# SS2D scan: the products with C made for two tiles at once, and two buffers shared

## The chip, the cores and the metric

The kernel runs on one core of one Trainium2 chip. The metric is the time of one whole execution in microseconds (us), the median of several runs. Before the change it is 18144.38 us (three runs, 18138.38 to 18144.7).

The core has five engines that run at the same time, each with its own queue of instructions that it works off in order: TensorE (PE in the profile; its weight loads are PEld), VectorE (DVE), ScalarE (ACT), GpSimd (POOL) and SyncE (SP), whose queue here issues the transfers between HBM and the on-chip memory.

## The reference

The network has four layers on eight images of 56 x 56 positions and 128 channels. Layers 0, 2 and 3 are deformable convolutions with a feed-forward part; the change does not touch them. Layer 1 is a vision state-space block. Its core is a selective scan with Di = 256 channels, N = 16 states per channel and K = 4 directions (rows forward, columns forward, and both reversed):

```
def step(h, t):
    dt_t, u_t, B_t, C_t = t
    h = h * jnp.exp(dt_t[..., None] * A) + (dt_t * u_t)[..., None] * B_t[:, :, None, :]
    y = jnp.einsum('bkdn,bkn->bkd', h, C_t)
    return (h, y)
...
_, ys = jax.lax.scan(step, h0, ts)
ys = ys + Ds.reshape(K, Di)[None, :, :, None] * xs
...
y = _ln(y, out_norm_w, out_norm_b)
y = y * jax.nn.silu(z)
y = jnp.einsum('bhwd,cd->bhwc', y, out_proj_w)
x = x + y
xm = _ln(x, norm2_w, norm2_b)
h = jax.nn.gelu(jnp.einsum('bhwc,fc->bhwf', xm, fc1_w) + fc1_b)
x = x + jnp.einsum('bhwf,cf->bhwc', h, fc2_w) + fc2_b
```

Here dt is a softplus of a projection, and B and C are rows per state that all channels share. So for each image, direction, channel and state, a first-order recurrence runs over 3,136 positions; each h is multiplied by C and summed over the 16 states.

## The kernel before

*Tiles and steps.* A step is one image, one direction and one chunk of SC = 784 positions: 8 images x 4 directions x 4 chunks = 128 steps, the directions in the order 1, 3, 0, 2. The 256 x 16 pairs of channel and state do not fit 128 partitions; a step is cut into 32 tiles t, each of 32 channels by 4 states. The tile's channel group is cg (8 of them) and its state group is sg (4 of them), and t = 4 cg + sg. "A group" in what follows is the four tiles of one cg. That makes 4,096 tiles in all.

*One tile's work*, in `scans` (L1323):
- `decay` (L1366): ScalarE computes dA = exp(dt * A) into one of two PSUM buffers.
- `spread` (L1358): once per group TensorE copies dt*x into PSUM (tile dtu, one buffer).
- `inputs` (L1371): u = dtu * B. For sg 0, 1 and 2 VectorE does it (two buffers u); for sg 3 GpSimd does it from on-chip memory, into the single buffer up.
- L1471: VectorE runs the recurrence (a tensor-tensor scan) into h, which has three buffers of one tile.
- L1474: ScalarE copies the last column into st, the carry to the next chunk (not in the last chunk of a direction).
- L1476: GpSimd multiplies h by the rows of C into hc, which has six buffers.
- `add_sums` (L1395): TensorE sums hc over the states into the PSUM bank acc, two tiles at a time, three tiles later. `open_sums` and `close_sums` begin and empty acc every eight tiles.

*What sets the order.* The program is unrolled in Python, in the order in which `scans` writes it; a scheduler then orders the instructions of each engine by this priority and by when it expects their inputs and buffers to be ready. `tc.issue_after` keeps the sums behind the last `spread` on TensorE. Waits come from data and from buffers: a new use of a buffer waits until everything that read the old one is done. So the scan of tile t waits for the product of tile t - 3 (three buffers h), and the product of tile t waits for the sums of tile t - 6 (six buffers hc).

*Background work.* While step `at` is scanned, a generator `prepare` (L1265) makes the next step's dt, B and C, one piece at each tile with sg 1 or 2: projections on TensorE, then for each half of the channels the softplus as Relu(x) + Ln(1 + Exp(-|x|)) on ScalarE (L1288 to L1292, the logarithm in tile sp, the rest in tile dd, one buffer each), an add and a product on GpSimd (L1294 and L1296), and a transfer of dd to HBM (L1298). `fetch_dt` (L1309) and `fetch_row` (L1301) bring dt and the rows of B and C back, spread over partitions; B and C have five buffers of one tile each, and the rows for the next step are fetched at tiles 25, 28, 29, 30 (B) and 26, 29, 30, 31 (C). A queue of tasks advances by one piece at most tiles: `input_stage` (L1110) prepares the next image (norm, convolution, gate; it writes tile pre), and `output_stage` (L1182) finishes an image in 8 pieces of 392 positions: it centers y into tile yc (L1195), normalizes it (L1203), gates it on GpSimd (L1207), projects it, and runs the feed-forward part in tile pre.

Of the kernel before, what the change touches and what calls it, by code (L numbers as in the profile page):

```python
# [41 lines left out]
F32 = mybir.dt.float32  # L42
# [70 lines left out]
NCH = DI // 128  # L113
XD = RANK + 2 * NST

LC = 448
NLC = L // LC
RPC = LC // W
SC, SR = 784, 14
# [4 lines left out]
NF = FF // 128  # L124
# [865 lines left out]
class Vss:  # L990
# [191 lines left out]
    def output_stage(self, i, c):  # L1182
# [4 lines left out]
        nc.sync.dma_start(out=sg, in_=self.gates[i][:, NCH:, m * c : m * (c + 1)])  # L1187
        yield
        yield
        yc = self.bg.tile([128, NCH, m], F32, name="yc", tag="yc")  # L1190
        for h in range(NCH):
            ps = self.misc()
            for g in range(NCH):
# [24 lines left out]
        nc.scalar.copy(x, ps[:, :m])  # L1218
        yield
        xT = self.bg.tile([128, m], F32, name="xT", tag="xT")  # L1220
        pre = self.bg.tile([128, NF, m], F32, name="pre", tag="pre", padded_shape=[128, NF, LC])
        ps = self.misc()
        nc.tensor.matmul(ps[:, :m], lhsT=w["center"], rhs=x, start=True, stop=True)
        nc.scalar.copy(xT, ps[:, :m])
# [39 lines left out]
    def prepare(self, s, k, c):  # L1264

        nc, w = self.nc, self.w
        xs = self.part(self.xb, k, c)
        dbl = self.prep.tile([XD, SC], F32, name="dbl", tag="dbl")
        s["rows"] = self.dram.tile([NST, 2 * SC], F32, name="rows", tag="rows")
        s["dd"] = self.dram.tile([DI, 2 * SC], F32, name="dds", tag="dds")  # L1270
        for b in range(2):
            ps = self.misc()
            for ch in range(NCH):
                nc.tensor.matmul(ps[:XD, :SH].rearrange("p (a b) -> p a b", b=W), lhsT=w["xproj"][:, ch, k, :], rhs=xs[:, ch, SR // 2 * b : SR // 2 * (b + 1)], start=ch == 0, stop=ch == NCH - 1)
            yield
            nc.scalar.copy(dbl[:, SH * b : SH * (b + 1)], ps[:XD, :SH])
        nc.sync.dma_start(out=s["rows"].rearrange("n (x e) -> (n x) e", x=2), in_=dbl[RANK:])
        yield
        for h in range(NCH):
            dd = self.prep.tile([128, 2, SC], F32, name="dd", tag="dd")  # L1280
            sp = self.prep.tile([128, SC], F32, name="sp", tag="sp")

            bias = w["dt_b"][:, NCH * k + h : NCH * k + h + 1]
            for b in range(2):
                at = slice(SH * b, SH * (b + 1))
                ps = self.misc()
                nc.tensor.matmul(ps[:, :SH], lhsT=w["dt"][:, k, 128 * h : 128 * (h + 1)], rhs=dbl[:RANK, at], start=True, stop=True)
                nc.scalar.activation(sp[:, at], ps[:, :SH], AF.Abs, bias=bias)  # L1288
                nc.scalar.activation(dd[:, 0, at], ps[:, :SH], AF.Relu, bias=bias)
                yield  # L1290
            nc.scalar.activation(sp, sp, AF.Exp, scale=-1.0)
            nc.scalar.activation(sp, sp, AF.Ln, bias=1.0)  # L1292
            yield
            nc.gpsimd.tensor_add(dd[:, 0], dd[:, 0], sp)  # L1294
            yield
            nc.gpsimd.tensor_mul(dd[:, 1].rearrange("p (a b) -> p a b", b=W), dd[:, 0].rearrange("p (a b) -> p a b", b=W), xs[:, h])  # L1296
            yield
            nc.sync.dma_start(out=s["dd"][128 * h : 128 * (h + 1)], in_=dd.rearrange("p x e -> p (x e)"))  # L1298
            yield

    def fetch_row(self, s, x, sg):  # L1301

        name = "bc"[x]
        t = s[name, sg] = self.work.tile([128, SC], F32, name=name, tag=name, bufs=NSG + 1)
        r = s["rows"]
        src = bass.AP(tensor=r.tensor, offset=r.offset + TS * sg * 2 * SC + x * SC, ap=[[0, TC], [2 * SC, TS], [1, SC]])
        self.nc.sync.dma_start(out=t, in_=src)
# [15 lines left out]
    def scans(self):  # L1323
# [99 lines left out]
        decay(*units[0])  # L1423
        inputs(*units[0])
        st = ready = None
        group, late = [], deque()
        zeros = self.zeros()
        for now, (at, t) in enumerate(units):
            (i, k, c), s, (cg, sg) = steps[at], state[at], order[t]
            forward = k < 2  # L1430
            if t == 0:
                if at % NSC == 0:
                    st = self.prep.tile([128, NT], F32, name="st", tag="st", bufs=2)
                    nc.gpsimd.memset(st, 0.0)
                if at % (NDIR * NSC) == 0 and i + 1 < self.images:
                    tasks.append(self.input_stage(i + 1))
                ready = iter(())
                if at + 1 < len(steps):
                    if steps[at + 1][0] > i:
                        self.load_xb(i + 1)  # L1440
                    ready = self.prepare(state[at + 1], *steps[at + 1][1:])
            if t % (2 * NSG) == 0:
                late.append((now + 5, open_sums, (at, t)))
            while late and late[0][0] <= now:
                _, do, args = late.popleft()
                do(*args)
            if sg == 1:
                to = divmod(NCG * at + cg + 2, NCG)
                if to[0] < len(steps):
                    self.fetch_dt(state[to[0]], to[1])  # L1450
            if t in (3, 19):
                next(zeros, None)

            for x, when in enumerate(((25, 28, 29, 30), (26, 29, 30, 31))):
                if t in when and at + 1 < len(steps):
                    self.fetch_row(state[at + 1], x, when.index(t))
            if now + 1 < len(units):
                decay(*units[now + 1])
                if not on_pool(units[now + 1][1]):
                    inputs(*units[now + 1])  # L1460

                if sg == NSG - 3 and now + 3 < len(units):
                    spread(*units[now + 3])
            if now + 2 < len(units) and on_pool(units[now + 2][1]):
                inputs(*units[now + 2])
            if sg in (1, 2):
                next(ready, None)
            hh = self.work.tile([128, SC], F32, name="h", tag="h", bufs=3)
            step = 1 if forward else -1
            u, dA = s.pop(("u", t)), s.pop(("dA", t))  # L1470
            nc.vector.tensor_tensor_scan(hh[:, ::step], dA[:, :SC][:, ::step], u[:, ::step], st[:, t : t + 1], ALU.mult, ALU.add)  # L1471
            if c != (NSC - 1 if forward else 0):
                last = SC - 1 if forward else 0
                nc.scalar.copy(st[:, t : t + 1], hh[:, last : last + 1])  # L1474
            hc = self.work.tile([128, SC], F32, name="hc", tag="hc", bufs=6)
            nc.gpsimd.tensor_mul(hc, hh, s["c", sg])  # L1476
            group.append((order[t], hc))
            if t % 2:
                late.append((now + 3, add_sums, (at, group)))
                group = []  # L1480
                if t % (2 * NSG) == 2 * NSG - 1:
                    late.append((now + 5, close_sums, (at, t)))
            if sg or (i == self.images - 1 and k == 2):
                advance(1)
# [81 lines left out]
```

## Time and profile before

| | |
|---|---|
| median of the runs | 18144.38 us |
| the profiled execution | 18131.72 us |
| its span, first to last instruction | 18130.2 us |
| scan stage within it, about | 2,360 to 13,500 us |
| busy DVE / POOL / PE / ACT, whole span | 15374.0 / 11790.9 / 13876.0 / 10917.1 us |
| product hc (L1476) | 4,096 of 1.877 us, 7559.1 us |
| scan h (L1471) | 3,072 of 1.838 and 1,024 of 1.833 us |
| u on VectorE (L1379) and up on GpSimd (L1375) | 3,072 of 0.955, 1,024 of 1.860 us |
| dA on ScalarE (L1369) | 4,096 of 0.915 us |
| add and product of the preparation (L1294, L1296) | 256 each, of 1.862 and 2.056 us |
| gating of y (L1207) | 64 of 1.852 us |
| a step in the scan stage, 3,000 to 13,000 us | about 87 us (115 steps) |

How to read it: a line of a group gives the line of the kernel, the engine, the operation, output and inputs by tile name with their shapes, the count, then the busy time and mean duration in ns of one, and after the second bar the engine's idle time just before these instructions with what ended it ("<-POOL hc L1476 260.8": for 260.8 us the engine waited until GpSimd's product ended). Durations of neighbours overlap by some 0.05 to 0.1 us, so the distance from start to start is a little shorter than the mean duration. In a table of stretches the columns are the stretch, its length, busy time and count of PE, PEld, DVE, ACT and POOL, the granted TensorE clock, the DMA share and GB/s.

### The profile page before, as it was taken

To read this page: it belongs to the slowest core of one execution; us is meant where nothing else is said; L and a number is where in the kernel's file an instruction comes from. 1 tells how busy PE (TensorE), PEld (TensorE's weight loads), DVE (VectorE), ACT (ScalarE), POOL (GpSimd) and SP (SyncE) were. 2 spreads that over 40 slices of the span, in tenths; PEclk is the share of its full clock that TensorE was granted. 3 is DMA by queue.
4 is the path that set the end of the run, shared out by engine and by line. 5 is a ranking of instruction groups with operands and counts; after the bars stand their busy time and mean duration, and the time that the engine had idled before them with its cause. 6 is when DMAs were issued, how large, how long until landed. Compare 5 with 4: busy or idle time off the path is not lost. (4 is left out here: it accounts for less than half of the span.)

```text
span 18130.2 us, 255599 instructions
## 1 busy us (share of the span) xinstructions
PE 13876.0 (77%) x90059; PEld 6901.9 (38%) x90059; DVE 15374.0 (85%) x17784; ACT 10917.1 (60%) x19602; POOL 11790.9 (65%) x6462
## 2 busy tenths in 40 slices
PE   5777787688688688688788778778676888577777
PEld 4655422233232232232223223222134666455555
DVE  8888368998998998998998898899976887688886
ACT  4666555566566566566566566656554666456666
POOL 2221079998998998998998998999971111222221
PEclk7778888899899899899899899889886888677777
DMA  7777444444443443444443444444335777577777
GB/s 216 210 200 206 133 146 157 160 170 154 146 158 139 143 160 137 147 157 142 141 159 139 148 156 141 143 156 149 138 120 141 198 199 197 148 203 202 203 200 174
DMA packets 1341766, 2961.81 MB, mean 163 GB/s; under 512 B 91168, under 2 KB 892132, under 8 KB 1325836
## 3 DMA queue, kind: packets, MB, share of 16 engines
q1 hardware_dynamic: 1340460, 2945.21, 52.4%
q8 instruction: 720, 11.80, 0.3%
q14 instruction: 586, 4.80, 0.1%
HBM read 2243.88 MB, written 866.92 MB: 172 GB/s over the span
## 5 line engine op out<-in xcount | busy, mean ns | idle before, releaser
L1476 POOL TENSOR_TENSOR hc<-h,c 128x784 f32<-128x784 f32 x4096 | 7559.1, 1877 | 594.7 <-DVE h L1471 348.4
L1471 DVE TENSOR_TENSOR_SCAN h<-dA,st,u 128x784 f32<-128x784 f32 x3072 | 5572.7, 1838 | 367.1 <-ACT dA L1369 190.2
L1369 ACT ACTIVATE dA<-dt,v_A 128x784 f32<-128x784 f32 x4096 | 3743.1, 915 | 864.5 <-DVE h L1471 852.9
L1401 PE MATMUL acc<-hc,v_sum 128*32 128x392 f32 x16384 | 3105.8, 533 | 141.4 <-POOL hc L1476 139.8
L1379 DVE TENSOR_TENSOR u<-dtu,b 128x784 f32<-128x784 f32 x3072 | 2860.7, 955 | 398.8 <-PE dtu L1363 390.7
L1363 PE MATMUL dtu<-dt,ident 128*128 128x392 f32 x4096 | 2012.8, 622 | 1221.8 <-issue 864.5
L736 POOL TENSOR_TENSOR ay<-hat,om 112x756 f32<-112x756 f32 (+2 forms) x192 | 516.2, 2688 | 2755.4 <-ACT hat L727 2359.4
L1471 DVE TENSOR_TENSOR_SCAN h<-dA,st,up 128x784 f32<-128x784 f32 x1024 | 1877.2, 1833 | 297.0 <-POOL hc L1476 278.1
L1375 POOL TENSOR_TENSOR up<-dt,b 128x784 f32<-128x784 f32 x1024 | 1904.6, 1860 | 65.9 <-DVE h L1471 33.4
L807 ACT COPY st<-pt 128x448 f32<-128x448 f32 (+1 forms) x2240 | 1175.8, 541 | 1218.2 <-PE pt L805 1211.3
L1474 ACT COPY st<-h 128x1 f32<-128x1 f32 x3072 | 583.5, 190 | 2047.5 <-DVE h L1471 2040.5
L775 DVE TENSOR_TENSOR win<-win,patch 112x252 f32 (+2 forms) x3456 | 1691.7, 502 | 125.8 <-DVE win L775 33.1
L805 PE MATMUL pt<-ident,sw 112*128 112x112 f32 (+2 forms) x8960 | 1609.8, 310 | 208.2 <-DMA sw<-skew 208.1
L1401 PEld LDWEIGHTS acc<-hc,v_sum 128*32 128x32 f32 x16384 | 758.1, 115 | 2547.2 <-issue 1630.8
L1363 PEld LDWEIGHTS dtu<-dt,ident 128*128 128x128 f32 x4096 | 848.3, 227 | 2251.6 <-issue 1348.9
L766 POOL MEMSET win<- 128x1820 f32 (+2 forms) x384 | 630.4, 1648 | 1461.4 <-DMA skew<-win 1156.3
L821 PE MATMUL yps<-st,xw 128*32 128x48 f32 (+5 forms) x35840 | 1076.4, 245 | 399.1 <-ACT st L807 396.3
L805 PEld LDWEIGHTS pt<-ident,sw 112*128 112x128 f32 (+2 forms) x8960 | 1119.5, 161 | 493.3 <-DMA sw<-skew 169.7
L772 DVE TENSOR_TENSOR patch<-ay,hat 112x756 f32<-112x756 f32 (+2 forms) x1152 | 1222.1, 1066 | 20.9 <-POOL ay L736 17.9
L821 PEld LDWEIGHTS yps<-st,xw 128*32 128x32 f32 (+2 forms) x35840 | 755.4, 125 | 827.2 <-ACT st L807 475.9
L725 ACT ACTIVATE hat<-om,taps 112x252 f32<-112x252 f32 x1280 | 755.7, 729 | 287.5 <-DVE patch L772 270.2
L1128 PE MATMUL misc<-xn,v_tap 128*128 128x448 f32 x2016 | 837.4, 563 | 64.0 <-ACT xn L1162 27.2
(193 smaller groups left out, 19611.3 us busy)
## 6 DMA issues: line engine op xcount, KB each, us to landing
dt<-dds SPq DMA_DIRECT2D x1024, 784.0 KB
b<-rows SPq DMA_DIRECT2D x512, 392.0 KB
c<-rows SPq DMA_DIRECT2D x512, 392.0 KB
dds<-dd SPq DMA_DIRECT2D x256, 784.0 KB
sw<-skew SPq DMA_DIRECT2D x224, 812.0 KB
sw<-skew SPq DMA_DIRECT2D x224, 672.0 KB
sw<-skew SPq DMA_DIRECT2D x224, 588.0 KB
xw<-table SPq DMA_DIRECT2D x224, 320.0 KB
```

Source lines behind the costliest of these rows:

```text
L772: nc.vector.tensor_mul(patch[:n], bcast(a, 3, KX), bcast(b, 2, KY))
L775: self.last_add = nc.vector.tensor_add(to, to, patch[:n, NCB * p : NCB * (p + 1)]).ins
L805: last = nc.tensor.transpose(ps[:m, n * g : n * (g + 1)], sw[:n, g, p : p + m], self.net.ident[:n, :n])
L807: nc.scalar.copy(st[:m], ps[:m, : G * n])
L821: self.nc.tensor.matmul(yps[CG * g : CG * (g + 1), t0:t1], lhsT=xw[:m, k + part, CG * g : CG * (g + 1)], rhs=st[:m, at + t0 : at + t1], st ...
L1363: last = nc.tensor.matmul(ps[:, b, :SH], lhsT=self.net.ident, rhs=s["dt", cg][:, 1, SH * b : SH * (b + 1)], start=True, stop=True)
L1369: nc.scalar.activation(da[:, :SC], s["dt", cg][:, 0], AF.Exp, scale=w["A"][:, k, NSG * cg + sg : NSG * cg + sg + 1])
L1375: nc.gpsimd.tensor_mul(u, s["dt", cg][:, 1], s["b", sg])
L1379: nc.vector.tensor_mul(halves[0], s["dtu", cg][:, :, :SH], halves[1])
L1401: nc.tensor.matmul(acc[r : r + TC, :SH], lhsT=w["sum"], rhs=hc[:, SH * b : SH * (b + 1)], start=False, stop=sg == NSG - 1)
L1471: nc.vector.tensor_tensor_scan(hh[:, ::step], dA[:, :SC][:, ::step], u[:, ::step], st[:, t : t + 1], ALU.mult, ALU.add)
L1476: nc.gpsimd.tensor_mul(hc, hh, s["c", sg])
```

## The change

Three edits go together.

1. h becomes a buffer of two tiles (two of them, four tiles of room instead of three). The scans of tiles 2p and 2p + 1 write its halves. After the second, GpSimd multiplies the whole pair, 128 x 1568 columns, by a pair buffer of C's rows, into a pair buffer hc (three of them, six tiles as before). `add_sums` gets the halves at the same place in the program. The rows of C lie in three pair buffers instead of five single ones; their fetches for the next step are written at tiles 26, 28, 31 and 31.
2. In `prepare` the logarithm's tile sp is gone; it uses the second half of dd, where the product for the scan's input is written later.
3. In `output_stage` the tile yc is gone; the centered y lies in the first half of pre, which is taken earlier for that.

The on-chip room that h and C gain is that of sp and yc.

```
-        yc = self.bg.tile([128, NCH, m], F32, name="yc", tag="yc")
+        pre = self.bg.tile([128, NF, m], F32, name="pre", tag="pre", padded_shape=[128, NF, LC])
+        yc = pre[:, :NCH, :]
...
-        pre = self.bg.tile([128, NF, m], F32, name="pre", tag="pre", padded_shape=[128, NF, LC])
...
-            sp = self.prep.tile([128, SC], F32, name="sp", tag="sp")
+            sp = dd[:, 1]
...
-        name = "bc"[x]
-        t = s[name, sg] = self.work.tile([128, SC], F32, name=name, tag=name, bufs=NSG + 1)
+        if x == 0:
+            t = s["b", sg] = self.work.tile([128, SC], F32, name="b", tag="b", bufs=NSG + 1)
+        else:
+            if sg % 2 == 0:
+                s["c", sg // 2] = self.work.tile([128, 2, SC], F32, name="c", tag="c", bufs=NSG // 2 + 1)
+            t = s["c", sg // 2][:, sg % 2]
...
-            for x, when in enumerate(((25, 28, 29, 30), (26, 29, 30, 31))):
-                if t in when and at + 1 < len(steps):
-                    self.fetch_row(state[at + 1], x, when.index(t))
+            for x, when in enumerate(((25, 28, 29, 30), (26, 28, 31, 31))):
+                for row in range(NSG):
+                    if t == when[row] and at + 1 < len(steps):
+                        self.fetch_row(state[at + 1], x, row)
...
-            hh = self.work.tile([128, SC], F32, name="h", tag="h", bufs=3)
+            if t % 2 == 0:
+                pair = self.work.tile([128, 2, SC], F32, name="h", tag="h", bufs=2)
+            hh = pair[:, t % 2]
...
-            hc = self.work.tile([128, SC], F32, name="hc", tag="hc", bufs=6)
-            nc.gpsimd.tensor_mul(hc, hh, s["c", sg])
-            group.append((order[t], hc))
             if t % 2:
-                late.append((now + 3, add_sums, (at, group)))
-                group = []
+                hc = self.work.tile([128, 2, SC], F32, name="hc", tag="hc", bufs=3)
+                nc.gpsimd.tensor_mul(hc, pair, s["c", sg // 2])
+                late.append((now + 3, add_sums, (at, [(order[t - 1], hc[:, 0]), (order[t], hc[:, 1])])))
```

In the order that the scheduler gives GpSimd, up of the next group stands between two groups' products in both kernels; it stands ahead of the last two products of the group before in 35 groups of the old order and in 167 of the new, out of 1,024.

More of the change, by code (lines that the diff above doesn't have):

```diff
@@ L1425, in scans @@
         st = ready = None
-        group, late = [], deque()
+        late = deque()
         zeros = self.zeros()
```

## The prediction

> **What bounds the kernel now.** First the page's busy shares and its 40 slices: only the selective scan (about 2,360 to 13,500 us) has work of GpSimd on the lines that change.
>
> ```profile
> PE 13876.0 (77%) x90059; PEld 6901.9 (38%) x90059; DVE 15374.0 (85%) x17784; ACT 10917.1 (60%) x19602; POOL 11790.9 (65%) x6462
> ...
> DVE  8888368998998998998998898899976887688886
> ...
> POOL 2221079998998998998998998999971111222221
> ```
>
> In slices 7 to 30 VectorE and GpSimd both stand at 8 or 9 tenths. Then the groups of instructions between 3,000 and 13,000 us, VectorE's and GpSimd's, with what ended the idle time before each:
>
> ```profile
> L1471 DVE TENSOR_TENSOR_SCAN h<-dA,st,u 128x784 f32<-128x784 f32 x2759 | 5004.8, 1838 | 329.3 <-ACT dA L1369 169.2 <-POOL hc L1476 56.4 <-POOL up L1375 7.6
> L1379 DVE TENSOR_TENSOR u<-dtu,b 128x784 f32<-128x784 f32 x2759 | 2569.4, 955 | 268.6 <-PE dtu L1363 264.6
> L1471 DVE TENSOR_TENSOR_SCAN h<-dA,st,up 128x784 f32<-128x784 f32 x920 | 1686.7, 1833 | 275.9 <-POOL hc L1476 260.8 <-ACT st L1474 8.3 <-ACT dA L1369 2.8
> ...
> L1476 POOL TENSOR_TENSOR hc<-h,c 128x784 f32<-128x784 f32 x3679 | 6788.9, 1877 | 522.6 <-DVE h L1471 299.2 <-PE acc L1401 197.5 <-PE dtu L1363 7.5
> L1375 POOL TENSOR_TENSOR up<-dt,b 128x784 f32<-128x784 f32 x919 | 1709.5, 1860 | 56.7 <-DVE h L1471 28.7 <-DVE u L1379 12.9 <-DMA b<-rows 8.4
> ```
>
> The reader sees what GpSimd costs VectorE: 56.4 + 7.6 + 260.8 = 325 us in these 115 steps (920 groups of four tiles), 2.83 us a step, 362 us over 128 steps. That is the ceiling of what a faster GpSimd can return directly. VectorE's other waits (dA 172 us, dtu 265 us) belong to ScalarE and TensorE. Third, the busy time of the four stretches of one image (directions 1, 3, 0 and 2, four steps each):
>
> ```profile
> 4088.00:4478.00 390.00, 331.32 (x1080) 114.23 (x1080) 321.40 (x245) 246.10 (x416) 334.04 (x188) 0.93 0.44 155
> 4478.00:4818.00 340.00, 246.03 (x934) 87.50 (x930) 314.65 (x229) 203.08 (x362) 331.36 (x186) 0.87 0.42 147
> 4818.00:5149.00 331.00, 244.86 (x966) 92.08 (x968) 315.30 (x230) 195.19 (x346) 318.24 (x176) 0.89 0.45 160
> 5149.00:5491.00 342.00, 288.98 (x1061) 106.50 (x1058) 318.47 (x268) 228.72 (x414) 326.14 (x177) 0.94 0.42 145
> ```
>
> After the span and its length stand the busy times of PE, PEld, DVE, ACT and POOL. GpSimd is busy 331.4 of 340 us in the second stretch: it is the bound there. In the third VectorE nearly is; the first has TensorE's convolution chunks and long waits for dtu. Last, instructions in order of time (start, duration, engine, line, operation). Four tiles of VectorE:
>
> ```profile
> 6010.02 0.94 DVE L1379 TENSOR_TENSOR u<-dtu,b 128x784 f32<-128x784 f32 x1
> 6011.10 1.85 DVE L1471 TENSOR_TENSOR_SCAN h<-dA,st,u 128x784 f32<-128x784 f32 x1
> 6012.86 1.83 DVE L1471 TENSOR_TENSOR_SCAN h<-dA,st,up 128x784 f32<-128x784 f32 x1
> 6014.60 1.83 DVE L1379 TENSOR_TENSOR u<-dtu,b 128x784 f32<-128x784 f32 x2
> 6016.35 3.58 DVE L1471 TENSOR_TENSOR_SCAN h<-dA,st,u 128x784 f32<-128x784 f32 x2
> 6019.85 0.95 DVE L1379 TENSOR_TENSOR u<-dtu,b 128x784 f32<-128x784 f32 x1
> ```
>
> GpSimd in the third stretch, where it waits for a scan once a group:
>
> ```profile
> 4827.61 3.69 POOL L1476 TENSOR_TENSOR hc<-h,c 128x784 f32<-128x784 f32 x2
> 4831.94 3.66 POOL L1476 TENSOR_TENSOR hc<-h,c 128x784 f32<-128x784 f32 x2 [0.63 <-DVE h L1471]
> 4835.55 1.84 POOL L1375 TENSOR_TENSOR up<-dt,b 128x784 f32<-128x784 f32 x1
> 4837.34 3.71 POOL L1476 TENSOR_TENSOR hc<-h,c 128x784 f32<-128x784 f32 x2
> ```
>
> VectorE repeats every 9.83 us (6010.02 to 6019.85). Counted from scan 0, scans start at 0, 1.75, 4.58 and 6.34, and scan 4 at 9.83. GpSimd needs 4 x 1.82 + 1.81 = 9.1 us, start to start, so it regains 0.7 us a group (the row's idle 0.63).
>
> **The change, part by part.**
> *Products in pairs.* 4,096 products of 784 columns become 2,048 of 1,568. What falls away is one instruction's fixed part per pair, which no row isolates. Low end: a GpSimd memset of one column takes 0.10 us. High end: its affine select of 128 columns takes 0.292, less at least 128 x 0.83 ns (slope between memsets of 1,484 and 2,268 columns, 1.338 and 1.990 us) is 0.19. I take 0.15, their middle: a pair is 3.65 - 0.15 = 3.50. A long product could also stream worse: single products range from 1.823 to 2.067 us, so the far end is 2 x 2.07 = 4.13.
>
> The Trainium skill, GPSIMD Engine Reference, section 3.1, has 2,048 columns at 4.497 us; with the trace's 784 in 1.825 a line gives 3.48 as an estimate, 348 us of GpSimd in all instead of my 307. The same section's 2.6 cycles an element speak against the change: 784 columns are 1.70 us of streaming as an estimate, so only 0.13 could be saved, 260 us. The trace can't yet say which.
>
> *The later start, and what GpSimd may lag.* A pair's product starts after its second scan, but scan 2p now waits for pair p-2. Before: product 0 ends at about 1.9 + 0.15 + 1.82 = 3.9 and scan 3 needs it at 6.34; slack 2.45. After: pair 0 starts at 3.65, ends 7.15, and scan 4 needs it at 9.83; pair 1 starts 8.2, ends 11.7, needed at 14.41; slack 2.65. GpSimd needs 2 x 3.50 + 1.81 = 8.81, so it regains 1.02 a group. Behind a waiting scan stand u, the carry copy and the next dA; behind a late product stand the sums on TensorE. Spread of the next group needs u 6 at 14.4, and the sums ahead of it need pair 0 at 7.15: hidden by 7 us. Products wait for sums three pairs back, as before (six tiles).
>
> *Bursts.* Twice a step GpSimd runs the preparation's add and product, 1.86 + 2.05 - 0.1 of overlap = 3.8 us; in half the steps also y's gating (64 of 128), 1.82.
> Before, per step: 3.8 - 2.45 = 1.35; three groups later 2.45 - 3 x 0.7 = 0.35 remains, so 1.70; gating paid in full, 0.91. Sum 3.96.
> After: 1.15; regained by the second burst, 1.15; gating 0.80 and 0.61 on the second burst, halved 0.70. Sum 3.0.
> The measured 2.83 is below 3.96, since other stalls let GpSimd catch up, so I use only the ratio, 0.76: 362 x 0.24 = 87 us gained. The second stretch, where GpSimd never catches up, can give up to 64 x 0.15 = 9.6 of its 15 us instead of the ratio's 3.6; I take 3 more for 8 images: 24.
>
> *Order.* On GpSimd's queue the next group's up (it needs the fourth scan) stood ahead of the second half of the products in 35 of 1,024 groups; in the new order it stands ahead of a finished pair in 167. There pair 1 ends 1.82 later, with 0.85 slack. Alone it is covered; beside a burst (60 of 256 in the new order), pair 0 ends at 9.75, pair 1 at 15.07 against 14.33: 0.74 more. 60 x 0.74 = 44 us lost.
>
> *c's rows.* The same 512 transfers of 392 KB. Rows 2 and 3 now both wait on SP's queue for pair 28/29 (7.15) instead of products 29 and 30 (5.6, 8.3), and are needed at 18.1 instead of 16.3 and 18.1: about 11 us as before, and GpSimd waited 2.1 us for c in the whole run. Next dt fetches are behind them on SP; they have two groups. Nothing; if the cover is gone, at most one late pair a step.
> *Shared buffers.* The logarithm in dd's second half makes ScalarE's Abs wait for the dds transfer; its neighbour Relu had that wait already (36 us of idle in those 115 steps). Centered y in pre waits for the previous pre, whose last readers are matmuls several yields earlier, or one gate transfer at the turn to an image's output: nothing, at most 8 x 10 us.
>
> Sum: -87 - 24 + 44 = -67 us against the profiled execution, 18131.72 us (span 18130.2), so 18065. That one is 12.7 below the median 18144.38; on the median's footing, 18077.
>
> **Rivals.**
> *GpSimd is the bound throughout*: the whole 2,048 x 0.15 = 307 us comes back (205 to 362, the ceiling): 17837, at best 17782. For it: the second stretch. Against: VectorE alone needs 8 x 9.83 = 78.6 of a step's 86.9 us, and 5 us of its waits are others'.
> *Hidden*: bursts cost the same, order eats the rest: 18110 to 18180.
> *Slower*, by the order on GpSimd's queue: if POOL is so late that each of 167 groups loses up's 1.82 us, +304 against -111: 18337. It decides from 111 / 1.82 = 61 groups. For it: the slack there is 0.85. Against: only 60 bursts lie there.
> *Not what it says*: a pair at 4.13 makes GpSimd 10.07 a group, 80.6 + 7.6 + 1.2 = 89.4 a step against 86.9: 18464. Against: the median single is 1.874, near its minimum.
>
> **How the numbers follow.** A repeated measurement tells 0.2%, 36 us. Forecast 0.44 (own range 17990 to 18108), bound throughout 0.10, hidden 0.18, order 0.24, slow pair 0.04. So faster 0.54, same 0.18, slower 0.28. 17900 to 18300 leaves out most of the second case and the tails of the last two, some 0.15.
>
> **What would show it.** Right: 2,048 products near 3.50 us; VectorE's waits for hc and up falling from 325 to about 260 us in the same 115 steps; scan waits now before even tiles instead of the up scan; the second stretch shortest by 5 us or more. Wrong: a pair above 3.65; scans waiting after up-before-pair groups; dtu or dA waits (265, 172) growing, which would mean that the later product holds TensorE or ScalarE.

## The result and the profile after

The changed kernel takes 18175.29 us (median of 20 runs, 18157.76 to 18197.84), the kernel before 18144.54 us beside it (20 runs, 18120.96 to 18160.65). The ratio is 1.0018, 95% interval 1.0011 to 1.0025. The forecast was 18077 us; the time moved by 31 us in the other direction, less than the 36 us that had been called telling, but clear of the interval. The profiled executions lie further apart than the medians: 18131.72 us before and 18196.48 us after, one of the slowest of its kernel, so the differences read from the two traces are somewhat larger than those between typical runs.

First the busy shares on the page of the changed kernel, and then the busy times between 3,000 and 13,000 us of the kernel before and of the changed one (columns: stretch, length, PE, PEld, DVE, ACT, POOL, granted clock, DMA share, GB/s).

```profile
PE 14024.5 (77%) x90059; PEld 6931.2 (38%) x90059; DVE 15358.9 (84%) x17784; ACT 10901.8 (60%) x19602; POOL 11533.0 (63%) x4414
```

```profile
3000.00:13000.00 10000.00, 7860.51 (x28536) 2793.78 (x28532) 9105.98 (x6886) 6181.98 (x10857) 9408.12 (x5187) 0.90 0.43 150
```

```profile
3000.00:13000.00 10000.00, 7974.90 (x28451) 2815.61 (x28450) 9048.90 (x6856) 6150.83 (x10822) 9135.46 (x3338) 0.91 0.43 149
```

GpSimd does get 258 us of work less (11790.9 to 11533.0), as meant. But VectorE gets 57 us less done in the same 10,000 us: it stands idle for longer. The groups of VectorE and GpSimd in that stretch, after the change, say for what:

```profile
L1478 DVE TENSOR_TENSOR_SCAN h<-dA,st,u 128x784 f32<-128x784 f32 x2747 | 4977.4, 1837 | 551.0 <-ACT dA L1373 264.0 <-POOL hc L1484 217.0 <-issue 1.7
L1383 DVE TENSOR_TENSOR u<-dtu,b 128x784 f32<-128x784 f32 x2746 | 2558.5, 955 | 326.3 <-PE dtu L1367 322.4
L1478 DVE TENSOR_TENSOR_SCAN h<-dA,st,up 128x784 f32<-128x784 f32 x915 | 1674.9, 1831 | 72.1 <-ACT dA L1373 37.8 <-POOL up L1379 24.0 <-POOL hc L1484 9.7
...
L1484 POOL TENSOR_TENSOR hc<-h,c 128x1568 f32<-128x1568 f32 x1832 | 6499.8, 3558 | 824.7 <-DVE h L1478 561.1 <-PE acc L1405 125.1 <-PE dtu L1367 76.4
L1379 POOL TENSOR_TENSOR up<-dt,b 128x784 f32<-128x784 f32 x916 | 1701.6, 1858 | 24.0 <-DVE h L1478 9.2 <-issue 5.8 <-POOL hc L1484 5.6
```

The scans' waits for GpSimd fell from 325 to 217.0 + 24.0 + 9.7 = 251 us, and they moved from the scan that reads up to the scans that open a pair. In exchange the scans' waits for dA rose from 172 to 264.0 + 37.8 = 302 us, and u's waits for dtu from 265 to 322 us: 74 us won, 187 lost. The net of 113 us is more than the 57 of lost work because smaller waits fell by 32 us, those for xt's transfer (20 to 1 us) and for st (10 to 1) the most, and gaps too short to be put down to any wait by some 25. GpSimd's own idle time ahead of products rose by 302 us (522.6 to 824.7), most of it waits for scans (299 to 561): the 289 us that its products save here come out as idle time.

Who makes dA and dtu late? The chain of waits, total over the same 10,000 us, first before, then after (columns: engine, tile and line, what it waited for, us, times, longest):

```profile
ACT sp L1288 <- PE misc L1287: 216.4, 212, 3.8
DVE h L1471 <- ACT dA L1369: 171.9, 172, 4.7
PE acc L1401 <- POOL hc L1476: 130.4, 143, 2.1
```

```profile
ACT dd L1288 <- PE misc L1287: 418.5, 178, 7.1
DVE h L1478 <- ACT dA L1373: 301.8, 309, 4.5
PE acc L1405 <- POOL hc L1484: 300.2, 149, 5.3
```

Read from below: TensorE's sums (acc) wait 170 us longer for the product; ScalarE's Abs in the preparation (L1288) waits 202 us longer for the dt projection of TensorE (L1287); the scans wait 130 us longer for dA of ScalarE. One burst of the preparation shows that these are links of one chain. The changed kernel in order of time (start, duration, engine, line, operation; in brackets the idle time before it and what ended it):

```profile
9146.98 1.84 POOL L1294 TENSOR_TENSOR dd<-dd 128x784 f32<-128x784 f32 x1
...
9148.90 1.85 POOL L1296 TENSOR_TENSOR dd<-dd,xb 128x784 f32<-128x784 f32 x1
...
9150.70 7.17 POOL L1484 TENSOR_TENSOR hc<-h,c 128x1568 f32<-128x1568 f32 x2
...
9154.37 2.49 PE L1405 MATMUL acc<-hc,v_sum 128*32 128x392 f32 x8 [2.49 <-POOL hc L1484]
...
9156.79 1.67 PE L1287 MATMUL misc<-dbl,v_dt 8*128 8x392 f32 x2
...
9158.55 0.59 ACT L1288 ACTIVATE dd<-misc,v_col 128x392 f32<-128x392 f32 x1 [5.78 <-PE misc L1287]
...
9159.58 0.93 ACT L1373 ACTIVATE dA<-dt,v_A 128x784 f32<-128x784 f32 x1
...
9160.60 1.85 DVE L1478 TENSOR_TENSOR_SCAN h<-dA,st,u 128x784 f32<-128x784 f32 x1 [1.79 <-ACT dA L1373]
...
9166.75 1.85 DVE L1383 TENSOR_TENSOR u<-dtu,b 128x784 f32<-128x784 f32 x2 [2.56 <-PE dtu L1367]
```

The add and the product of the preparation hold GpSimd from 9146.98 to 9150.70. The first pair is then done only at 9154.3, 3.6 us later. TensorE has stood for it for 2.49 us, because the sums of that pair are next in its queue; the dt projection, which needs nothing of them, is written behind them and comes at 9156.79. ScalarE stands 5.78 us at Abs, with the exponential dA for the next scans behind it; so VectorE stands 1.79 us for dA. The 2.56 us more for dtu come over TensorE alone: `spread` stands behind the projection and some matmuls of the output stage, which are all late. A part of this lateness is TensorE's clock, granted at half from 9154.75 to 9164.99. The same place before the change:

```profile
9132.03 7.40 POOL L1476 TENSOR_TENSOR hc<-h,c 128x784 f32<-128x784 f32 x4
...
9133.97 1.85 DVE L1471 TENSOR_TENSOR_SCAN h<-dA,st,up 128x784 f32<-128x784 f32 x1 [1.12 <-POOL hc L1476]
...
9135.83 0.85 PE L1401 MATMUL acc<-hc,v_sum 128*32 128x392 f32 x4 [1.00 <-POOL hc L1476]
...
9136.73 0.92 PE L1287 MATMUL misc<-dbl,v_dt 8*128 8x392 f32 x2
9137.75 0.59 ACT L1288 ACTIVATE sp<-misc,v_col 128x392 f32<-128x392 f32 x1 [0.89 <-PE misc L1287]
```

There the first product came 1.9 us after the burst, so TensorE could sum half and stood 1.00 us for the other half; Abs stood 0.89 us, and VectorE's one wait in this stretch is 1.12 us. The clock is at half here too, but for less long (9138.43 to 9141.84). The queue order on TensorE is the same in both kernels here.

Over the whole program the scheduler did move something: of the dt projections' 1,024 matmuls 778 stand behind as many sums as before, 242 stand earlier in TensorE's queue. That does not make the effect: of the 202 us by which Abs's waits rose, 142 (168 to 310) are at those whose place is unchanged. The link from Abs to the scans is looser. By a rough count over the trace (the longest stop of ScalarE among the eight instructions ahead of a late dA), Abs stands behind 7 us of the waits for dA before and 71 after, about half of the rise; copies of other results of TensorE (dbl and xn) stand behind 31 and 84.

The four stretches of that image after the change:

```profile
4107.00:4497.00 390.00, 326.68 (x1055) 114.01 (x1054) 317.05 (x242) 240.38 (x412) 320.90 (x120) 0.93 0.43 150
4497.00:4833.00 336.00, 250.99 (x928) 88.62 (x928) 312.40 (x228) 202.04 (x362) 321.02 (x117) 0.87 0.43 150
4833.00:5164.00 331.00, 255.26 (x980) 93.49 (x981) 317.31 (x232) 196.62 (x350) 312.12 (x115) 0.91 0.46 160
5164.00:5510.00 346.00, 292.91 (x1077) 104.73 (x1075) 319.84 (x270) 232.47 (x418) 322.23 (x117) 0.95 0.43 146
```

The prediction named these stretches wrongly, as directions 1, 3, 0 and 2. The bounds are memsets of st, which run one direction ahead, so they are 3, 0, 2 and direction 1 of the next image. Mean lengths after the first image: 382.5 to 379.8, 338.5 to 337.1, 331.6 to 335.7, and 343.2 to 348.0 us. The first two, with the longest waits for GpSimd, gain a little; the last two, which hold most of the output stage (three gatings of y an image each, where the first two have one), lose more. By the waits of VectorE an image, GpSimd gave back about 4, 2, 2 and 3.5 us in the four, while dA and dtu together took 6, 3.5, 6 and 11 more; that the first two gain all the same lies in smaller waits and is not resolved here.

### The profile page after: what moved, and what is told of

It reads as the page before. It is cut to its first block, busy times and chain, and to the rows that moved or that the text cites. A ratio compares the mean times of both kernels' runs of the same rounds, so it can differ in the third digit from the quotient of the medians.

```text
span 18194.8 us, 251069 instructions
## 1 busy us (share of the span) xinstructions
PE 14024.5 (77%) x90059; PEld 6931.2 (38%) x90059; DVE 15358.9 (84%) x17784; ACT 10901.8 (60%) x19602; POOL 11533.0 (63%) x4414
## 5 line engine op out<-in xcount | busy, mean ns | idle before, releaser
L1484 POOL TENSOR_TENSOR hc<-h,c 128x1568 f32<-128x1568 f32 x2048 | 7267.1, 3558 | 937.2 <-DVE h L1478 645.8
L1405 PE MATMUL acc<-hc,v_sum 128*32 128x392 f32 x16384 | 3307.7, 539 | 320.7 <-POOL hc L1484 318.8
L1367 PE MATMUL dtu<-dt,ident 128*128 128x392 f32 x4096 | 1974.8, 611 | 1065.3 <-issue 692.8
L1405 PEld LDWEIGHTS acc<-hc,v_sum 128*32 128x32 f32 x16384 | 809.7, 115 | 2838.3 <-issue 2003.0
```

The source lines that it names most:

```text
L1367: last = nc.tensor.matmul(ps[:, b, :SH], lhsT=self.net.ident, rhs=s["dt", cg][:, 1, SH * b : SH * (b + 1)], start=True, stop=True)
L1405: nc.tensor.matmul(acc[r : r + TC, :SH], lhsT=w["sum"], rhs=hc[:, SH * b : SH * (b + 1)], start=False, stop=sg == NSG - 1)
L1484: nc.gpsimd.tensor_mul(hc, pair, s["c", sg // 2])
```

## The experiments

Two theories are told apart. A: the product comes later and in one piece, and TensorE's queue hands that on (sums, then dt projection, then Abs and dA on ScalarE). B: the shared buffers cost what the pairs win. Each experiment starts from the kernel before or the changed one. In the table the waits are those between 3,000 and 13,000 us, and each ratio is to runs of the kernel before that lay beside it (medians 18138 to 18145). "Abs" is ScalarE's wait for the dt projection alone; with the logarithm in dd it also waits for GpSimd itself, 68 us in the changed kernel, 102 in e1, 189 in e2 and 161 in e9.

| kernel | median us | ratio to before, 95% | scans for GpSimd | scans for dA | u for dtu | sums for GpSimd | Abs |
|---|---|---|---|---|---|---|---|
| before | 18144.54 | | 325 | 172 | 265 | 130 | 216 |
| changed | 18175.29 | 1.0018 [1.0011, 1.0025] | 251 | 302 | 322 | 300 | 418 |
| e1 shared buffers only | 18152.81 | 1.0006 [0.9997, 1.0015] | 301 | 183 | 272 | 109 | 129 |
| e8 changed, own logarithm | 18176.78 | 1.0022 [1.0013, 1.0031] | 260 | 301 | 309 | 282 | 431 |
| e2 changed, two products | 18122.77 | 0.9991 [0.9982, 1.0000] | 180 | 223 | 352 | 149 | 142 |
| e9 the same, second half written first | 18155.07 | 1.0008 [0.9999, 1.0017] | 189 | 242 | 351 | 157 | 149 |
| e3 changed, sums a tile later | 18100.11 | 0.9976 [0.9967, 0.9985] | 290 | 274 | 233 | 309 | 442 |
| e4 changed, preparation a piece later | 18060.14 | 0.9953 [0.9939, 0.9966] | 225 | 156 | 295 | 245 | 245 |
| e5 before, preparation a piece later | 18125.06 | 0.9996 [0.9987, 1.0005] | 298 | 156 | 298 | 97 | 195 |
| e6 changed, both later | 18132.44 | 0.9995 [0.9986, 1.0004] | 213 | 135 | 385 | 224 | 219 |
| e7 = e4 with two products | 17995.51 | 0.9924 [0.9911, 0.9938] | 177 | 155 | 309 | 136 | 202 |
| e12 four single tiles h | 18079.58 | 0.9965 [0.9951, 0.9979] | 55 | 263 | 384 | 194 | 156 |
| e10 = e12, preparation later | 17970.99 | 0.9908 [0.9893, 0.9924] | 67 | 203 | 327 | 149 | 232 |
| e11 five single tiles h | 17971.36 | 0.9909 [0.9894, 0.9924] | 83 | 193 | 341 | 165 | 235 |

**The shared buffers.** e1 is the kernel before with edits 2 and 3 alone:

```
-            sp = self.prep.tile([128, SC], F32, name="sp", tag="sp")
+            sp = dd[:, 1]
...
-        yc = self.bg.tile([128, NCH, m], F32, name="yc", tag="yc")
+        pre = self.bg.tile([128, NF, m], F32, name="pre", tag="pre", padded_shape=[128, NF, LC])
+        yc = pre[:, :NCH, :]
```

> Edits 2 and 3 alone: single products, three buffers h, five c, six hc as before; the logarithm in dd's second half and centered y in pre. Theory A (the pair's product starts after its second scan and ends late; the sums that wait for it hold TensorE's queue, the dt projection behind them is late, ScalarE stands at Abs with the next dA behind it): nothing of that is in this kernel, so 18130 to 18155 us, VectorE's waits for dA near 172 us and for dtu near 265 us in the same 115 steps. Theory B (the shared buffers hold ScalarE, since Abs now waits for what only Relu waited for): 18170 us or more, waits for dA near 300 us.

It runs as before (8 us slower, within its interval). e8 is the changed kernel with the first of these two edits undone:

> The changed kernel with the logarithm in its own tile sp again (centered y still shares pre; both own tiles together need 1 KB a partition more than there is). Theory A: 18165 to 18185 us, waits for dA near 300 us, ScalarE's idle time before Abs for the projection near 400 us. Theory B, as far as the logarithm goes: back to 18145 us or below and waits for dA near 172 us.

Nothing changes either: 18176.78 against 18175.29 us. And e2 below has both shared buffers and is faster than the kernel before. B is out.

**Merged or not, and the later start.** e2 keeps pair buffers and all else of the change, but makes two products, each right after its scan; e9 writes the same two after the second scan, in the other order, so that both should begin after it:

```
-                nc.gpsimd.tensor_mul(hc, pair, s["c", sg // 2])
+            nc.gpsimd.tensor_mul(hc[:, t % 2], hh, s["c", sg // 2][:, sg % 2])    # e2, at each tile
...
+                for x in (1, 0):                                                   # e9, written after the second
+                    nc.gpsimd.tensor_mul(hc[:, x], pair[:, x], s["c", sg // 2][:, x])
```

> All of the change but the merged instruction: pair buffers for h, c and hc, and the shared buffers, but GpSimd multiplies each tile of 784 columns as soon as its own scan is done (4,096 products). Theory A: the first half of each pair's sums is early again, TensorE's idle time for hc goes from 302 back to about 130 us and VectorE's waits for dA from 302 to about 180 us in 115 steps; scans wait for GpSimd a little less than before, since h now holds four tiles; 18090 to 18140 us. Theory B: the shared buffers are still there: 18170 us or more, dA near 300 us. A third (the pair buffers' release is what costs, not the late product): also 18170 us or more, with VectorE waiting for hc.

> The changed kernel with two products of 784 columns, the second half first: both start only after the pair's second scan, as the merged product does, but nothing is merged. It separates the later start from the merging. Theory A (the later start is the price, the merging saves some): the later start stays and the saving of about 0.17 us a pair is given back, so it is slower than the changed kernel's 18175 us: 18180 to 18300 us, TensorE's idle time for hc at 302 us in 115 steps or more. If it were the length of one instruction (its result comes in one piece): as e2, 18110 to 18140 us.

e2 kept to its range of time, but not to its waits: dA fell to 223 us, not 180, and dtu rose to 352. e9 did not test what it was made for. The scheduler undid the written order: in the trace the first product of a pair begins before the pair's second scan has ended in 911 of 2,048 pairs (914 in e2; in none of the changed kernel), and the order of the instructions is that of e2 on every engine, but for 6 of TensorE's 90,059 places. In these lines of e9 the second scan (of up) of a pair runs from 4023.84, and the first product starts at 4024.07:

```profile
4022.07 1.85 DVE L1478 TENSOR_TENSOR_SCAN h<-dA,st,u 128x784 f32<-128x784 f32 x1 [0.40 <-ACT dA L1373]
4023.84 1.82 DVE L1478 TENSOR_TENSOR_SCAN h<-dA,st,up 128x784 f32<-128x784 f32 x1
...
4024.07 3.75 POOL L1485 TENSOR_TENSOR hc<-h,c 128x784 f32<-128x784 f32 x2 [1.16 <-DVE h L1478]
```

So what e9 shows is something else. It is e2 in another build, and it takes 32 us more (18122.77 to 18155.07). With it goes a product that takes 1.873 us on the mean instead of 1.856 (1.877 in the kernel before, 1.876 in e1); why, no run says. Two kernels that differ by some 30 us may thus differ for a reason other than the order of the work, and that holds for the 31 us between the kernel before and the changed one too. Firmer are the forecast gain of 67 us that did not come, and the waits, which are much alike in e2 and e9.

With that caution: the rest of the change without merging wins 30 us on e1 (18152.81 to 18122.77), for which four tiles of room for h are the likely reason, since the scans' waits for GpSimd fall from 301 to 180 us. Merging costs 52 us against e2 and 20 against e9, although it makes GpSimd's work shorter. The waits in e2, to be set beside those of the changed kernel above:

```profile
DVE h L1478 <- ACT dA L1373: 223.0, 260, 3.7
DVE h L1478 <- POOL hc L1484: 157.3, 125, 5.8
PE acc L1405 <- POOL hc L1484: 149.1, 124, 2.8
ACT dd L1288 <- PE misc L1287: 141.9, 132, 3.5
```

The merged product doubles the sums' waits (149 to 300 us) and nearly triples Abs's for the projection (142 to 418; Abs's idle time of all causes goes from 381 to 543). The scans wait 79 us more for dA and 71 more for GpSimd, more than half of the 120 by which e2 lies below e1; their waits for dtu do not rise (352 to 322). The merged product both starts later and hands on its result in one piece; no run separates the two.

**TensorE's queue.** e3 writes each pair's sums one tile later; e4 writes one empty piece into the preparation, which shifts its projections, its work on ScalarE and its burst on GpSimd by one place against the scans:

```
-                late.append((now + 3, add_sums, ...))
+                late.append((now + 4, add_sums, ...))        # e3 and e6
...
         dbl = self.prep.tile([XD, SC], F32, name="dbl", tag="dbl")
+        yield                                                # e4 to e7, e10, e11
```

> The changed kernel with the sums of a pair written one tile later (now + 4 instead of now + 3). Theory A: TensorE reaches the late sums later and waits less for hc (302 us to under 200 us in 115 steps), the dt projections come earlier in its queue, and VectorE's waits for dA and dtu fall by some 100 us together: 18080 to 18150 us. But a product needs the sums of three pairs back, so GpSimd's idle time for acc may rise above 125 us. Theory B: no difference, 18165 to 18185 us.

> The changed kernel with one more empty piece at the beginning of the preparation, so that all its pieces are written one tile with sg 1 or 2 later. In GpSimd's order of the regular steps the add and product of the preparation then stand between the two pairs of a group instead of ahead of its first pair. Theory A: the first pair's product no longer ends 3.8 us late, the sums and the dt projection follow in time, waits for dA fall below 250 us in 115 steps: 18100 to 18160 us. Theory B: no difference, 18165 to 18185 us.

e3 is faster by 75 us, but not in the way that A said: the sums' waits (309) and Abs's (442) stay, and only u's waits for dtu fall (322 to 233). Nor does it test A: the scheduler put the sums nearly where they were. In the trace `spread` stands behind as many sums as in the changed kernel in all but 13 of 1,024 groups, and so do 838 of the projections' 1,024 matmuls. Where the 75 us come from is open. e4 gains 115 us, 40 more than its range allowed, and its waits are as A asks:

```profile
PE acc L1406 <- POOL hc L1485: 244.7, 142, 4.1
ACT dd L1289 <- PE misc L1288: 244.5, 145, 6.6
DVE h L1479 <- POOL hc L1485: 191.5, 152, 2.3
DVE h L1479 <- ACT dA L1374: 156.0, 216, 3.5
```

Abs waits 174 us less than in the changed kernel and the scans wait 146 us less for dA. In GpSimd's queue the first burst of a step now stands behind the pair of tiles 12 and 13 in 64 of 128 steps (in the changed kernel ahead of it, in 56), the second behind that of tiles 24 and 25 in 71 (ahead of it, in 77). This fits A, since there the pair that TensorE needs next is not delayed by the burst. But e4 moves the projections and ScalarE's work as well, so it does not isolate the burst.

> The kernel before with the empty piece of e4 at the beginning of the preparation, nothing else. It asks whose the gain of e4 is. If the place of the add and product alone made it (theory C: both kernels lose by the burst ahead of a group's first product, whatever the product's width), this gains about as much as e4 did against the changed kernel, 18144 - 115 = 18030 us. If the pairs are what the place frees (theory A: only the pair is late enough to hold TensorE), 18110 to 18150 us: waits for dA near 172 us already, scans' waits for GpSimd stay near 325 us in 115 steps.

> The changed kernel with both: the preparation one piece later (e4) and the sums one tile later (e3). e3 took 75 us off, mostly in waits for dtu (322 to 233 us in 115 steps), e4 115 us, mostly in waits for dA (302 to 156). If these are two different waits, they add up: 17980 to 18020 us. If both only give TensorE the same room, no better than e4: 18050 to 18070 us.

> e4 with two products of 784 columns instead of one of 1,568, into the same pair buffers: what the merged instruction is worth once its burst no longer holds TensorE. Theory A: the merged one saves 0.15 to 0.2 us a pair on an engine that still makes scans wait, so this is slower than e4 by 40 to 120 us: 18100 to 18180 us. If the fourth tile of h was the gain and the merging nothing, the same as e4, 18050 to 18070 us.

In the kernel before the same shift is worth 13 us against the kernel itself and 28 against e1. That does not make the late merged product the reason why it pays: it is worth 115 us with merged products, but 127 with two products in pair buffers (e2 to e7) and 109 with four single tiles (e12 to e10, below). It pays where h has four tiles, merged or not. e6 shows that e3's and e4's gains do not add; together they lose most of e4's (18132.44), with the longest waits for dtu of all (385 us). Why is open. e7 missed its expectation: merging is no gain of 40 to 120 us when the preparation lies better, but a loss of 65 us (17995.51 to 18060.14). Here the scans' waits for dA and u's for dtu are about the same with and without merging (155 and 156, 309 and 295 us); those for GpSimd rise from 177 to 225. So the price of merging is not paid over TensorE's queue alone: the scans also wait for the longer pair itself.

**Room without pairs.** e10 takes the kernel before, the two shared buffers, the shifted preparation and four single tiles of h; e11 five; e12 is e10 with the preparation where it was:

```
-            hh = self.work.tile([128, SC], F32, name="h", tag="h", bufs=3)
+            hh = self.work.tile([128, SC], F32, name="h", tag="h", bufs=4)
```

> No pairs at all: the kernel before with both shared buffers, the preparation one piece later (as e4 and e7) and the room spent on a fourth single buffer h. Against e7 (pair buffers, two products) it frees each tile by itself: the scan of every tile waits for the product of four tiles back. Theory A with the room as the gain: as e7 or a little better, 17960 to 18010 us, scans' waits for GpSimd at or below e7's 177 us in 115 steps. If the gain of e7 came from the pair buffers' form and not from the room: near e5, 18110 to 18140 us.

> As e10 with five single buffers h (c stays at five, so the room is the same as the changed kernel's). If scans still wait for GpSimd in bursts, a fifth tile takes up to 1.8 us more of each burst: 17920 to 17990 us, waits for GpSimd below 120 us in 115 steps. If four tiles cover the bursts, no better than e10 within 0.1%.

> The kernel before with the two shared buffers and four single tiles of h; products, rows of C, sums and preparation as before. It completes the square of room (three or four tiles of h) and place of the preparation (as before, or one piece later): three as before 18152 (run e1), three later 18125 (run e5), four later 17971 (run e10). If the two gains simply add, four alone is worth 18125 - 17971 = 154 us and this comes to about 18000. If the fourth tile is worth something only with the preparation moved, because without that the dt projection and ScalarE's Abs stand behind the late products, it is near the kernel with two products in pair buffers, 18123 (run e2): 18090 to 18140, with VectorE's waits for GpSimd below 180 us in 3,000 to 13,000 us and its waits for dA and dtu at 220 and 340 or more.

e10 is the fastest of all, 0.9908 [0.9893, 0.9924] of the kernel before. VectorE's groups in it:

```profile
L1472 DVE TENSOR_TENSOR_SCAN h<-dA,st,u 128x784 f32<-128x784 f32 x2812 | 5103.9, 1839 | 292.6 <-ACT dA L1370 166.5 <-POOL hc L1477 16.2 <-ACT st L1475 9.0
L1380 DVE TENSOR_TENSOR u<-dtu,b 128x784 f32<-128x784 f32 x2811 | 2622.1, 957 | 329.3 <-PE dtu L1364 326.6
L1472 DVE TENSOR_TENSOR_SCAN h<-dA,st,up 128x784 f32<-128x784 f32 x938 | 1717.5, 1831 | 96.5 <-POOL up L1376 47.1 <-ACT dA L1370 37.0 <-ACT st L1475 7.5
```

The scans' waits for products, 56.4 + 260.8 us in the kernel before, are 16.2 us here and 3 more: GpSimd is hardly faster (busy 11741.3 instead of 11790.9 us in the whole run), but its lag behind a burst is held by one more buffer. A fifth tile adds nothing. e12 ended 10 us below its range and completes a square. With three tiles (e1, e5) or four (e12, e10), preparation as before: 18152.81 and 18079.58; shifted: 18125.06 and 17970.99. The fourth tile alone is worth 73 us, the shift alone 28, both 182, so 81 us are only there together (e5 has its own buffers for the logarithm and y; against its own base, the kernel before, the shift is worth 13). With room alone GpSimd's waits are gone (55 us) but VectorE waits for dA (263) and dtu (384) instead, and the shift takes 59 and 58 of these away. Four single tiles also beat two pair buffers with the same two products, by 43 us (e2 to e12) and 25 (e7 to e10); a pair buffer comes free only when both its halves have been read, which fits, but no run isolates it, and e2 and e9 lie as far apart without any such difference.

## Why the prediction was wrong, and where it was right

- **The price of a pair: right.** It took 3.50 us a pair, 0.15 saved. From start to start, back to back, a pair takes 3.50 us on the mean (389 cases) and a single 1.826 (2,406 cases in the kernel before), so 0.15 is saved. The value was the middle between two bounds, so its exactness is luck. The Trainium skill, GPSIMD Engine Reference, section 3.1, had allowed, as estimates, 0.13 us by its cycles an element and 0.17 by its figure for 2,048 columns; 0.15 lies between them, and mean durations (2 x 1.877 - 3.558) give 0.20, so the runs don't decide between them.
- **Slack, bursts and the scans' waits for GpSimd: right in the sum.** It named about 260 us of 325 in the 115 steps; it was 251. The waits also moved to the scans that open a pair, as said. How the sum comes about it did not see: four tiles without merging bring the waits down to 180 us (e2), and merging brings them up again.
- **The step that failed** is in the part on the later start: "behind a late product stand the sums on TensorE. Spread of the next group needs u 6 at 14.4, and the sums ahead of it need pair 0 at 7.15: hidden by 7 us." That looked at one instruction behind the sums and at a group without a burst, and priced the late product at nothing. In a burst the pair is late by 3.8 us of preparation and by another 1.8 because the whole pair must end; and behind the sums stands not only `spread`, but the dt projection, on which ScalarE's queue, with dA in it, waits. Against the same kernel with two products (e2), the merged one has the sums waiting 300 instead of 149 us in 10,000, Abs 418 instead of 142, the scans 302 instead of 223 for dA and 251 instead of 180 for GpSimd, and costs 52 us of time (20 against e9). Against the kernel before, dA and dtu took 187 us where GpSimd gave back 74; but that is not all the merged product's doing, since e2 has dtu at 352 us and dA above the 172 as well. How much the later start costs and how much the one piece stays open.
- **The frame allowed the mistake.** "VectorE's other waits (dA 172 us, dtu 265 us) belong to ScalarE and TensorE" counted them as constants. They move with the product and with the room for h: over all kernels run, dA between 135 and 302 us, dtu between 233 and 385. The last sentence of the prediction named exactly this as the sign of its failure, but gave it no price and no chance; the rival on the slower side was up's order on GpSimd instead.
- **Order on GpSimd (+44): not confirmed.** Waits for up rose by 16 us only (7.6 to 24.0), and e4, which is 115 us faster, has up ahead of a finished pair about as often: in 178 groups by its trace, 186 in the changed kernel. (By the traces both counts named ahead of the result, 35 and 167, are too low: in the kernel before up stands ahead of the last product in 35 groups and ahead of the last two in another 49.) No run undoes that order alone. A slip in the sum: pair 1 is needed at 14.41 in one place and at 14.33 in another; with the first, 44 us would be 40.
- **The second stretch** gained 1.4 us an image, where 3.6 plus 3 was forecast: it is the stretch where GpSimd was the bound, but its own idle time grew there as everywhere (busy 331.36 to 321.02 us in the lines shown); a pair can't start before its second scan, which fits.
- **C's rows and shared buffers: right, nothing.** Waits of the product for C are 0.5 us (2.1 before); e1 and e8 bound the buffers within 10 us. But the room that they gave was part of the change, and that is worth up to 30 us in e2 and 73 as a fourth single tile (e12), a gain that the prediction saw only as slack of 2.65 instead of 2.45 us, since merging gives more than half of it back (251 us of waits against 180 in e2 and 301 in e1).
- **Rivals.** "Bound throughout" (17837) and "slow pair" (18464) are out by the profile. "Hidden" (18110 to 18180) holds the time as a number, though by another mechanism: bursts did cost less, and the waits behind the merged product ate it.

## What to carry to other kernels

Merging two instructions saves the fixed part of one (here 0.15 us a pair), but starts the first half later and hands on the result in one piece; before counting the saving, follow the result through every in-order queue that it enters, and ask what unrelated work is written behind its reader. Where an engine only lags in bursts, one more buffer for its input holds the lag: here a fourth tile of h was worth 73 us, and the merged product cost 20 to 65 in the three comparisons made. Waits that name another engine are not constants of a change; the burst in order of time, not the totals, shows whether they hang on the same late thing. And an experiment that reorders the program has to be read in the trace before its time is: the scheduler undid e9's order and most of e3's.

## What the runs showed of the hardware that was not expected

In every kernel with the merged product (changed, e3, e4, e6, e8) TensorE's sums take 200 to 201 ns of busy time each; in all others 189 to 192 ns (before: 2775.8 us for 14,712; changed: 2946.5 for 14,650). The groups of TensorE, before and after:

```profile
L1401 PE MATMUL acc<-hc,v_sum 128*32 128x392 f32 x14712 | 2775.8, 531 | 132.0 <-POOL hc L1476 130.4
```

```profile
L1405 PE MATMUL acc<-hc,v_sum 128*32 128x392 f32 x14650 | 2946.5, 538 | 302.0 <-POOL hc L1484 300.2
```

Waits of over 1 us for a product just ahead of sums number 14 before, 112 after, 32 in e2 and 40 in e9. In the burst shown, the granted clock after such a wait is half for 10 us, and eight sums take 2.49 us instead of the 1.51 at 9150.37, the projection 1.67 instead of 0.92:

```profile
9141.50:9154.50 13.00, 9.18 (x41) 3.00 (x41) 12.52 (x11) 8.04 (x17) 12.84 (x6) 1.00 0.24 84
...
9151.34:9154.75 3.41, 0.92 (x8) 0.17 (x6) 3.41 (x5) 1.01 (x2) 3.41 (x2) 1.00 0.94 329
...
9154.80:9165.00 10.20, 8.99 (x24) 4.51 (x21) 7.60 (x5) 3.90 (x8) 10.20 (x5) 0.50 0.23 74
```

The Trainium skill, TensorE: Matmul & The Clock Gate, section "What's actually happening", has the clock halved after an idle window of about 3.4 us. Here 2.49 us of standing were followed by half clock 0.4 us after the sums had begun, so a shorter wait was enough. The traces show how: in both, the granted clock is full or half and changes only on a grid of 3.41 us. Between 3,000 and 13,000 us TensorE was busy for under four tenths of 192 such windows at full clock before and of 237 after, and half clock followed each; it was busy for over nine tenths of 1,066 and 1,112, and half clock followed none. In between it was either. The window that ended with this drop, 9151.34 to 9154.75, holds 0.92 us of work. Only part of the sums' extra time is of this kind: 31 of the 112 groups ran wholly at half clock (2.83 us for eight; the other 81 took 1.81 on the mean), all 112 together took 65 us longer than at 1.51, and the mean granted clock of the whole stretch did not fall (0.90 before, 0.91 after). The rest of the longer busy time stays open.
